# Batches in groups of 2, 4, 4, 4, 2 with a table for each group, in a two-layer graph kernel

## The chip, the core and the metric

The kernel runs on one core of a Trainium2 chip. The time is device microseconds of one execution; the median of three timed runs is given, and lower is better. One more execution was recorded by the hardware profiler, and all views below are of that one. Engines: PE multiplies matrices, DVE is VectorE, ACT is ScalarE, POOL is GpSimd and issues the indirect DMAs (gathers and scatters), SP issues the plain DMAs.

## What is computed

There are 16 graphs ("batches") of 1024 nodes with 64 channels, `x` (16, 1024, 64), and a sparse weighted adjacency `adj` (16, 1024, 1024), 64 MB in float32. Most nodes have few neighbours; nodes with a low number have many, up to some 88. Two layers:

```python
h = relu(layernorm(x));  x = x + (adj / max(rowsum(adj), 1)) @ h              # layer 0
h = relu(layernorm(x))                                                       # layer 1
adj_d = dilate(adj)     # in rows with over 10 neighbours, every skip-th one is removed, on both sides
agg   = 0.25*q25 + 0.5*q50 + 0.25*q75 of h over the neighbours in adj_d      # per node and channel
x = x + (relu((h + agg) @ W1 + b1) @ W2 + b2) * mask
```

Layer 1 needs, per node and channel, a sort of a list whose length differs from node to node.

## The kernel before

**Layer 0** streams the adjacency once, batch by batch, in 8 row tiles of 128 x 1024. For each tile PE transposes it (`transposes`), ACT copies the transposed blocks out (`turned`) and takes the sign of every entry (`signs`), DVE multiplies the signs by column keys and takes the eight largest of each of four interleaved segments (`listing`, MAX8), which gives the list of neighbours. PE then multiplies (`products`), DVE adds the residual, and `channels` makes the normed rows of layer 1, which SP writes to a table in DRAM: one table `tab` for all 16 batches, 1025 rows each, with one row of huge values for empty places.

`endings` gives every node of a batch a place in the order of list lengths (`to`, DVE) and scatters its record (normed row, residual, list) to that place of the group's DRAM tensor `srt[g]`: 8 indirect DMAs of POOL for a batch.

**A group** is four batches (`GB`). When all four are scattered, `group(g)` loads the records sorted by length as 32 tiles of 128 nodes. Tile 0 holds the longest lists of every batch, and is left to `long_lists`. For the other 31, `CAPS` says how many neighbours each holds: 15, 10, 8, 7, 7, 6, and so on down to 1. The group also fetches 128 adjacency rows (`gat_rows`), scans them, and writes with two small scatters ("drops") into the table what each of the longest nodes removes; the gathers of layer 1 must see that.

**A job** (`Job`) takes the tiles of one cap, T of them, with n - 1 neighbours: POOL gathers one neighbour for 128 nodes with each indirect DMA (`places`), DVE works out which are removed (`rem`, `gone`, `ok`, `valid`) and the weights (`q`, `wu`, `w`), adds a huge value to removed ones, and runs a sorting network of `tensor_tensor` min and max between `places` and `other`; the result is weighted (`prod`), summed by PE, run through the two small matrices (`layers`) and scattered to the output by POOL (`out_dram`). Four `places` buffers exist. With `helped`, ACT adds the huge value and does part of the weighting, in pieces of 64 elements; before, that is so once all 16 batches are done.

**Long lists** (`long_lists`) are four jobs with 88, 31, 24 and 20 neighbours for 8 nodes of each batch, after layer 0. They gather from `tab` too (`lplaces`).

**The order.** All this is written as generators ("streams"). A planner (`Plan`) keeps a clock for every engine and for DMA, estimates when each tile is ready (`note`, `ready`, `used`), and always emits the stream that can begin earliest, with ranks to break ties. On DVE and POOL the instructions run in exactly the order in which the planner emits them; a wait at the head of POOL's queue holds everything behind it. `SLACK`, `LOOSE` and `LATE` are what it adds to be safe. An indirect DMA is reckoned with 1.27 us on POOL and 2.2 us to landing. The helper through which the planner records instructions is line 226, so most lines of the profile have that line, and tiles tell them apart.

Since the planner reckons `ready` and `used` for the table as a whole, a gather seems to it to wait for the latest row written by layer 0, and the next write of layer 0 for the latest gather.

Of the kernel before, what the change touches and what calls it, by code (L numbers as in the profile page):

```python
# [18 lines left out]
P = 128  # L19
# [8 lines left out]
GB = 4  # L28
SUB = 32
# [4 lines left out]

CAPS = (
    [0, 15, 10, 8, 7, 7, 6] + [5] * 4 + [4] * 4 + [3] * 6 + [2] * 6 + [1] * 5
)
LONG = (88, 31, 24, 20)
# [193 lines left out]
class Plan:  # L232
# [4 lines left out]
    def __init__(self, nc):  # L237
        names = {"vector": "DVE", "scalar": "ACT", "tensor": "PE", "gpsimd": "POOL", "sync": "SP"}
        self.nc = SimpleNamespace(
            **{attr: Timed(self, name, getattr(nc, attr)) for attr, name in names.items()}  # L240
        )
        self.clock = dict.fromkeys([*names.values(), "DMA"], 0.0)
        self.ready, self.used, self.users = {}, {}, {}
        self.slots, self.streams = {}, []
        self.last = self.own = None

# [21 lines left out]
    def note(self, engine, op, args, kwargs):  # L268
        if self.own is not None:
            self.clock[engine] = max(self.clock[engine], self.own)  # L270
        out = kwargs["out"] if "out" in kwargs else args[0]
        rest = [*args[0 if "out" in kwargs else 1:], *(v for k, v in kwargs.items() if k != "out")]
        rest = [getattr(v, "ap", v) if type(v).__name__.startswith("Indirect") else v for v in rest]
        rest = [v for v in rest if isinstance(v, bass.AP)]
        size = max(math.prod(v.shape[1:]) for v in (out, *rest[:2]))
        start = max(
            self.clock[engine],
            *(self.ready.get(v.tensor.name, 0.0) for v in rest if self.own is None),
            self.used.get(out.tensor.name, 0.0) if self.own is None else 0.0,
        )  # L280
        after = 0.15
        if engine == "DVE":
            half = op == "tensor_tensor" and all(v.dtype == HF for v in (out, *rest))
            time = 0.04 if op == "memset" else 0.07 + size * (0.57e-3 if half else 1.04e-3)
        elif engine == "ACT":
            pointers = sum(isinstance(kwargs.get(k), bass.AP) for k in ("bias", "scale"))
            time = 0.06 + size * 0.86e-3 + 0.11 * pointers + 0.09 * ("accum_out" in kwargs)
        elif engine == "PE":
            time = 0.1 + math.prod(out.shape[1:]) * 0.88e-3
            if op == "matmul" and rest[0].dtype == F32:  # L290
                time *= 2
        elif engine == "POOL":
            time, after = (1.27, 2.2) if op == "indirect_dma_start" else (0.15, 0.1)
            self.last = None
        else:
            start = max(start, self.clock["DMA"])
            rate = 165e3 if 4 * out.shape[-1] >= 512 else 85e3
            time, after = 0.05, 2.2 + math.prod(out.shape) * 4 / rate
            self.clock["DMA"] = start + after - 2.2
        self.clock[engine] = end = start + time  # L300
        self.ready[out.tensor.name] = end + after
        for v in rest:
            self.used[v.tensor.name] = max(self.used.get(v.tensor.name, 0.0), end + after)
        if "accum_out" in kwargs:
            self.ready[kwargs["accum_out"].tensor.name] = end + after
        return start
# [59 lines left out]
def list_path(ctx, tc, x, adj, nodemask, w1, b1, w2, b2, out, go):  # L366
# [7 lines left out]
    NG = B // GB  # L374
# [7 lines left out]
    NTAU = N // SUB  # L382
# [45 lines left out]
    which = consts.tile([P, 2], I32, name="which")  # L428
    nc.vector.tensor_scalar(which[:, 1:2], part, 3, None, op0=OP.logical_shift_right)
    nc.vector.tensor_scalar(which[:, 0:1], which[:, 1:2], GB - 1, None, op0=OP.bitwise_and)  # L430
    toff = consts.tile([P, 2], F32, name="toff")
    nc.vector.tensor_scalar(toff, which, float(TS), None, op0=OP.mult)
    noff = consts.tile([P, 2], F32, name="noff")
    nc.vector.tensor_scalar(noff, which, float(N), None, op0=OP.mult)
    caps = consts.tile([P, NTAU], F32, name="caps")
    for t, cap in enumerate(CAPS):
        nc.vector.memset(caps[:, t:t + 1], float(cap if t else N))
# [28 lines left out]
    tab = dram.tile([B * TS, W], F32, name="tab")  # L466
    srt = [dram.tile([GB * N, RW], F32, name=f"srt{g}") for g in range(NG)]
# [3 lines left out]
    nc.sync.dma_start(tab.rearrange("(b t) w -> b t w", t=TS)[:, N, :], none)  # L471
    pairs = tab.rearrange("r (a two) -> (r a) two", two=2)
# [5 lines left out]
    plan = Plan(nc)  # L478
    nc = plan.nc
# [224 lines left out]
    def channels(pool, now):  # L704

        for b, st in enumerate(batch):
            now[0] = b
            row = lambda: st["row"]
            yield "DVE", lambda: known(st, "row") if st["residual"] == 2 else INF
            yield from normed(row()[:, :, :C], row()[:, :, X1:R0])  # L710
            nc.sync.dma_start(
                tab[b * TS:b * TS + N, :].rearrange("(t p) w -> p t w", p=P), row()[:, :, :W]
            )
            st["normed"] = True

    def endings(pool, now):

        first = lambda rank: rank - 3000
        for b, st in enumerate(batch):
            now[0] = b  # L720
            g, gb = divmod(b, GB)
# [20 lines left out]
            for s in STEPS[1:]:  # L742
# [26 lines left out]
            nc.vector.tensor_scalar(low, low, LSUB - 1, None, op0=OP.bitwise_and)  # L769
            nc.vector.tensor_scalar(  # L770
                pos, pos, float(GB), float(LSUB * gb), op0=OP.mult, op1=OP.add
            )
            to = new(pool, [P, NT], I32, "to", 2)
            nc.vector.scalar_tensor_tensor(to, low, float(1 - GB), pos, op0=OP.mult, op1=OP.add)
# [26 lines left out]
    class Job:  # L801
# [3 lines left out]
        def __init__(self, pool, n, T, keys, idx, node, mask, nodes_i, table, S, g, name="places",  # L805
                     bufs=4, rank=0):
# [3 lines left out]
        def run(self):  # L810
# [6 lines left out]
                at(self.idx), room(self.name, self.bufs), room("S", 4) if short else 0.0  # L817
# [8 lines left out]
            for t in range(T):  # L826
                for k in range(n - 1):
                    if t or k:
                        yield "POOL", pace, *own
                    since.append(since[0] if since else plan.clock["POOL"])  # L830
                    gather(A[:, k + 1, t, :], self.table, self.idx[:, t, k:k + 1])
                    progress["ahead"] -= 1
# [17 lines left out]
        def sort(self):  # L850
# [31 lines left out]
            helped = progress["batches"] == B  # L882
# [82 lines left out]
            helped = progress["batches"] == B  # L965
# [41 lines left out]
        def layers(self, terms, sources):  # L1007
# [55 lines left out]
            for t in range(T):  # L1063
                yield "POOL", lambda: at(y) + LATE
                scatter(out_rows, y[:, t, :], self.nodes_i[:, t:t + 1], scatters)
# [3 lines left out]
    def group(g):  # L1069


        yield "SP", lambda: 0.0 if progress["batches"] >= (g + 1) * GB and (
            g < 2 or progress["jobs"][g - 2] == len(set(CAPS[1:]))
        ) else INF
        R = (g + 1) * GB
        table = tab[:R * TS, :]
        recs = new(grp, [P, NTAU, REC], F32, "recs", 2)
# [8 lines left out]
            nodes, node, noff[:, 0:1], float(g * GB * N), op0=OP.add, op1=OP.add  # L1086
        )
        nodes_i = new(grp, [P, NTAU], I32, "nodes_i", 2)
# [7 lines left out]
        found = new(grp, [P, N], BF, "gfound", 1).rearrange("p (t e) -> p t e", t=NTAU)  # L1096
# [7 lines left out]
        nc.vector.memset(over[:, 0:1], 0.0)  # L1104
        big = tiny.tile([P, NTAU], F32, name="big")
        nc.vector.tensor_tensor(big, m, caps, OP.is_gt)
# [3 lines left out]
        base = tiny.tile([P, 1], F32, name="gbase")  # L1110
        nc.vector.tensor_scalar(base, toff[:, 0:1], float(g * GB * TS), None, op0=OP.add)
# [6 lines left out]
        keys = new(grp, [P, NTAU, 16], F32, "keys", 2)  # L1118
        nc.vector.memset(keys, 0.0)
        left = tiny.tile([P, 8 * NSEG], F32, name="left")  # L1120
        for t in range(1, NTAU):
            nc.vector.max(out=keys[:, t, :8], in_=lists[:, t, :])
            if CAPS[t] > 8:
# [7 lines left out]

        assert all(cap <= T_THRESH for cap in CAPS[2:])
        skip = dilation(m[:, 1:2], mask[:, 1:2], 1)
        hit = tiny.tile([P, 2, 16], F32, name="hit")
        for e in range(2):
# [3 lines left out]
            nc.vector.tensor_tensor(hit[:, e, :], hit[:, e, :], keys[:, 1, :], OP.mult)  # L1139
        nc.vector.tensor_reduce(drop[:, 1, :], hit, AX.X, OP.add)  # L1140
        nc.vector.tensor_scalar(
            drop[:, 1, :], drop[:, 1, :], -1.0, float(N), op0=OP.mult, op1=OP.add
        )
        for e in range(2):
            nc.vector.tensor_tensor(keys[:, 1, :], keys[:, 1, :], hit[:, e, :], OP.subtract)
        didx = new(tiny, [P, 2], I32, "didx", 2)
        index_of(didx, node[:, 0:2], float(PW), basep)
        idx = new(grp, [P, NTAU, 16], I32, "idx", 2)
# [17 lines left out]
        for e in range(2):  # L1166
            nc.gpsimd.indirect_dma_start(
                out=pairs[:R * TS * PW, :],
                out_offset=bass.IndirectOffsetOnAxis(ap=didx[:, e:e + 1], axis=0),
                in_=drop[:, e, :], in_offset=None,  # L1170
            )
        classes = []
        for t in range(1, NTAU):
            if classes and CAPS[t] == CAPS[classes[-1][0]]:
# [3 lines left out]
        for i, ts in enumerate(classes):  # L1178
            n, T = CAPS[ts[0]] + 1, len(ts)
# [3 lines left out]
                nodes_i[:, sl], table, tiles[:, sl, :R0], g,  # L1183
            )
# [3 lines left out]
    def long_lists(pool):  # L1188
# [4 lines left out]
        for l, K in enumerate(LONG):  # L1193
# [3 lines left out]
            n32 = GB * LSUB  # L1197
            for g in range(NG):
                nc.sync.dma_start(
                    S[g * n32:(g + 1) * n32, 0, :], srt[g][l * n32:(l + 1) * n32, :]  # L1200
# [57 lines left out]
            for e in range(2):  # L1258
# [9 lines left out]
                pool, n, 1, keys, idx.unsqueeze(1), node, mask, nodes_i, tab, S, NG,  # L1268
                *(("lplaces", 2) if l else ("lplaces0", 1)), -600 + l,
# [4 lines left out]
    for g in range(NG):  # L1274
# [10 lines left out]
    with tc.tile_pool(name="long", bufs=1) as pool:  # L1285
        plan.add(long_lists(pool), -1500)
# [293 lines left out]
```

## Time and profile before

| | |
|---|---|
| median of 3 runs | 1524.7 us (1523.92 to 1529.08) |
| profiled execution | 1525.97 us, span 1523.8 us |
| DVE busy | 1211.9 us (80%), 4119 instructions |
| POOL busy | 960.8 us (63%), 931 indirect DMAs among 1156 instructions |
| ACT busy | 752.9 us (49%) |
| PE busy | 751.5 us (49%) |
| DMA | 129.01 MB, mean 85 GB/s |
| last scatter of rows (end of layer 0) | issued at 790.9 us |

Issue time on POOL isn't counted as busy, so a POOL that never stops shows some 75 to 80%. The slices of the page are 38.1 us each.

### The profile page before, as it was taken

The page shows a single profiled execution, that of the slowest core. Times are in us where ns is not written, and L with a number is a line of the kernel's source. Part 1 is how long each engine was busy: PE and PEld are TensorE (multiplying, and loading weights), DVE is VectorE, ACT ScalarE, POOL GpSimd, SP SyncE. Part 2 cuts the span into 40 slices and gives each one's busy share as a digit, 9 for nine tenths or more (in the row PEclk, how much of TensorE's full clock was granted, in tenths as well). Part 3 has the DMA queues.
Part 4 walks back from the last instruction along what each step waited for, and adds up shares of the span by engine and source line. Part 5 has one row for each costly group of instructions (what it writes and reads, how often), then busy time and mean ns, then how long its engine had stood idle before and what let it go on. Part 6 is the DMA issues. An engine that isn't in the chain of part 4 may idle for free. (4 is left out here: it accounts for less than half of the span.)

```text
span 1523.8 us, 15747 instructions
## 1 busy us (share of the span) xinstructions
PE 751.5 (49%) x3192; PEld 469.3 (31%) x3192; DVE 1211.9 (80%) x4119; ACT 752.9 (49%) x2503; POOL 960.8 (63%) x1156
## 2 busy tenths in 40 slices
PE   4887776576348777655825420013000056706454
PEld 2443342344214453432413320012000034605343
DVE  6878798999997699999734779995189999998852
ACT  7989878476436665675515320011410147516442
POOL 0122237745567766556677776567777777777774
PEclk8889987787568778767865655555555556857666
DMA  4555764455514354643322131221111111112110
GB/s 153 172 163 156 185 187 116 131 134 172 113 40 104 114 144 129 161 131 83 87 52 37 29 78 34 50 41 31 33 23 24 26 27 30 37 30 45 36 27 17
DMA packets 135536, 129.01 MB, mean 85 GB/s; under 512 B 100696, under 2 KB 103384, under 8 KB 135432
## 3 DMA queue, kind: packets, MB, share of 16 engines
q1 hardware_dynamic: 102696, 86.46, 20.6%
q0 software_dynamic: 32736, 41.47, 12.6%
q14 instruction: 76, 0.62, 0.1%
q8 instruction: 28, 0.46, 0.1%
HBM read 108.57 MB, written 19.28 MB: 84 GB/s over the span
## 5 line engine op out<-in xcount | busy, mean ns | idle before, releaser
L226 POOL DMA_INDIRECT places<-tab,idx x496 | 495.0, 998 | 161.2 <-issue 142.3
L226 PE MATMUL pt<-ident,prod 128*128 128x128 f32 (+1 forms) x736 | 159.1, 376 | 454.0 <-DVE prod L226 369.6
L226 PEld LDWEIGHTS pt<-ident,prod 128*128 128x128 f32 (+1 forms) x736 | 129.4, 257 | 486.1 <-ACT prod L226 287.8
L226 PE MATMUL ps_small<-att,h 128*65 128x512 f32 x512 | 255.4, 649 | 26.9 <-ACT h L226 22.4
L226 POOL DMA_INDIRECT srt<-row,to x128 | 129.6, 1013 | 208.8 <-ACT row L226 186.7
L226 PE MATMUL pt<-ident,at 128*128 128x128 f32 x1024 | 181.0, 324 | 106.7 <-ACT att L226 79.2
L226 POOL DMA_INDIRECT lplaces<-tab,lidx x163 | 166.9, 1024 | 53.7 <-issue 49.1
L226 PEld LDWEIGHTS pt<-ident,at 128*128 128x128 f32 x1024 | 138.5, 166 | 154.2 <-ACT att L226 104.8
L226 DVE MAX8 rec<-sg 128x8 f16<-128x256 f16 x512 | 180.1, 414 | 4.4
L226 ACT ACTIVATE sg<-at 128x1024 f16<-128x1024 f32 x128 | 135.1, 1056 | 69.4 <-DMA at<-in_adj_dram 48.8
L226 ACT COPY att<-pt 128x512 f32<-128x512 f32 x256 | 141.4, 583 | 28.4 <-PE pt L226 27.3
L226 POOL DMA_INDIRECT out_dram<-y,nodes_i x124 | 121.8, 983 | 37.9 <-issue 20.0
L226 PEld LDWEIGHTS ps_small<-att,h 128*65 128x65 f32 x512 | 75.7, 153 | 166.8 <-issue 127.6
L226 ACT ACTIVATE gone<-gone 128x18 f32<-128x18 f32 (+9 forms) x23 | 4.8, 208 | 234.1 <-DVE ok L226 234.1
L226 DVE TENSOR_TENSOR sg<-sg,keyed 128x1024 f16<-128x1024 f16 x128 | 87.4, 683 | 30.4 <-ACT sg L226 30.4
L226 DVE TENSOR_TENSOR long_other<-lplaces 128x512 f32<-128x512 f32 (+5 forms) x124 | 63.8, 557 | 21.8 <-ACT lplaces L226 21.6
L226 PE MATMUL ps_small<-ot,w_sb 128*128 128x128 f32 (+3 forms) x112 | 53.1, 564 | 53.3 <-ACT ot L226 22.5
L226 ACT COPY ot<-pt 128x128 f32<-128x128 f32 (+3 forms) x56 | 22.2, 396 | 109.6 <-PE pt L226 109.3
L226 DVE TENSOR_TENSOR other<-places,other 128x64 f32<-128x64 f32 (+6 forms) x204 | 69.6, 341 | 5.9
L226 ACT ACTIVATE places<-places,gone 128x64 f32<-128x64 f32 x283 | 70.7, 335 | 0.4
L226 ACT ACTIVATE prod<-places,w 128x64 f32<-128x64 f32 x157 | 39.5, 335 | 63.1 <-DVE w L226 63.1
L226 DVE TENSOR_TENSOR places<-places,other 128x64 f32<-128x64 f32 (+2 forms) x208 | 62.4, 310 | 4.9
(210 smaller groups left out, 1643.3 us busy)
## 6 DMA issues: line engine op xcount, KB each, us to landing
at<-in_adj_dram SPq DMA_DIRECT2D x128, 512.0 KB
places<-tab,idx POOLq DMA_INDIRECT x496, 2.5
tab<-row SPq DMA_DIRECT2D x16, 264.0 KB
xt<-in_x_dram SPq DMA_DIRECT2D x16, 256.0 KB
lplaces<-tab,lidx POOLq DMA_INDIRECT x163, 2.5
recs<-srt SPq DMA_DIRECT2D x4, 544.0 KB
srt<-row,to POOLq DMA_INDIRECT x128, 2.7
out_dram<-y,nodes_i POOLq DMA_INDIRECT x124, 2.2
```

The source lines that it names most:

```text
L226: ins = getattr(self._engine, op)(*args, **kwargs)
```

## The change

1. **Groups.** Five groups of 2, 4, 4, 4 and 2 batches. A group of two has 16 tiles; its first tile is shared, half for long lists and half for short ones of cap 15 (`HP`, `half`, `aside`), and its caps are `CAPS2`. There are 48 jobs of short lists instead of 40. The preparation of the last group is added with the long lists, after layer 0.
2. **A table for each group** instead of one `tab`, and `whole`, a copy of all of them that only the long lists gather from. SP copies each group's table there after the group's drops have landed (DRAM to DRAM). In a group of two one drop is enough.
3. **The plan.** A gather is put down at POOL's clock, without waiting for its table; writes of a table's parts neither wait for one another nor move its `ready`; DMA with small pieces keeps the DMA clock busy for half as long.
4. **`helped`** now holds for any job for which ACT's clock is less than 2 us ahead of DVE's, during layer 0 too.

```diff
-GB = 4
-SUB = 32
+GROUPS = (2, 4, 4, 4, 2)
...
+CAPS2 = [CAPS[1]] + CAPS[2::2]
...
         after = 0.15
+        apart = engine == "SP" and out.tensor.name in self.parts
+        if apart:
+            start = max(self.clock[engine], *(self.ready[v.tensor.name] for v in rest))
...
-            rate = 165e3 if 4 * out.shape[-1] >= 512 else 85e3
-            time, after = 0.05, 2.2 + math.prod(out.shape) * 4 / rate
-            self.clock["DMA"] = start + after - 2.2
+            busy = math.prod(out.shape) * 4 / 165e3
+
+            time, after = 0.05, 2.2 + busy * (1 if 4 * out.shape[-1] >= 512 else 2)
+            self.clock["DMA"] = start + busy
         self.clock[engine] = end = start + time
-        self.ready[out.tensor.name] = end + after
+        if not apart:
+            self.ready[out.tensor.name] = end + after
...
-    tab = dram.tile([B * TS, W], F32, name="tab")
-    srt = [dram.tile([GB * N, RW], F32, name=f"srt{g}") for g in range(NG)]
+    tabs = [dram.tile([n * TS, W], F32, name=f"tab{g}") for g, n in enumerate(GROUPS)]
+    whole = dram.tile([B * TS, W], F32, name="whole")
+    srt = [dram.tile([GROUPS[g] * N, RW], F32, name=f"srt{g}") for g in range(NG)]
...
+            if size == 2:
+                aside = new(tiny, [P, 2, NT], F32, "aside", 2)
+                for e, by in enumerate((-32.0, 64.0)):
+                    nc.vector.tensor_scalar(
+                        aside[:, e, :], pos, 64.0 / (e + 1), by, op0=OP.is_lt, op1=OP.mult
+                    )
+                for e in range(2):
+                    nc.vector.tensor_tensor(pos, pos, aside[:, e, :], OP.add)
...
+                    plan.own = plan.clock["POOL"]
                     gather(A[:, k + 1, t, :], self.table, self.idx[:, t, k:k + 1])
+                    plan.own = None
...
-            helped = progress["batches"] == B
+            helped = plan.clock["ACT"] < plan.clock["DVE"] + 2.0
...
-        for e in range(2):
-            nc.gpsimd.indirect_dma_start(
-                out=pairs[:R * TS * PW, :],
+        for e in range(2 if four else 1):
+            if e:
+                nc.gpsimd.memset(turn, 0.0)
+            ins = nc.gpsimd.indirect_dma_start(
+                out=table.rearrange("r (a two) -> (r a) two", two=2),
                 out_offset=bass.IndirectOffsetOnAxis(ap=didx[:, e:e + 1], axis=0),
                 in_=drop[:, e, :], in_offset=None,
             )
+            if e:
+                tc.declare_no_dep(ins.ins, other, reason="rows of their own")
+            other = ins.ins
+        dropped = at(table)
+        yield "SP", lambda: dropped
+        nc.sync.dma_start(whole[FIRST[g] * TS:R * TS, :], table)
...
-    for g in range(NG):
+    for g in range(NG - 1):
         plan.add(group(g), -2000)
...
     with tc.tile_pool(name="long", bufs=1) as pool:
+
+        plan.add(group(NG - 1, pool, "last_"), -2000)
         plan.add(long_lists(pool), -1500)
```

## The prediction

> **What bounds the kernel now.** I read the page's busy shares and slices first, then the waits of POOL and of VectorE, then POOL's timeline, whose rows I counted. The slices:
>
> ```profile
> DVE  6878798999997699999734779995189999998852
> ACT  7989878476436665675515320011410147516442
> POOL 0122237745567766556677776567777777777774
> ```
>
> POOL is empty in the first 65 us, and from slice 20 on it stands at 7 of 10 without a gap. Seven tenths is its full pace, as the timeline shows (start, duration, idle time before):
>
> ```profile
> 1082.49 0.94 POOL L226 DMA_INDIRECT lplaces<-tab,lidx  x1 [0.30 <-issue]
> 1083.73 0.95 POOL L226 DMA_INDIRECT lplaces<-tab,lidx  x1 [0.30 <-issue]
> 1084.99 0.94 POOL L226 DMA_INDIRECT lplaces<-tab,lidx  x1 [0.30 <-issue]
> ```
>
> One indirect DMA costs a slot of 1.25 us, 0.94 busy and 0.30 of issue. Summed over all 931, with the small memsets between scatters, slots take 1,222 us, 1.307 each; real waits take the other 302 us: 162 us before time 200, 97 from 200 to 800, 43 after. So after layer 0 the queue of POOL sets the end, and before it whatever makes gathers available.
>
> ```profile
> POOL srt L226 <- ACT row L226: 186.7, 24, 64.7
> POOL tab L226 <- DVE deg L226: 17.5, 1, 17.5
> POOL gat_rows L226 <- DVE nodes_i L226: 14.6, 1, 14.6
> ```
>
> These are POOL's longest waits: scatters that wait for a batch's rows (132 of the 186.7 us before time 200), then the preparation of the first group. The first group's gathers start at 214.7, because four batches must be sorted first (last scatter at 174.1):
>
> ```profile
> 174.14 0.96 POOL L226 DMA_INDIRECT srt<-row,to  x1 [0.19 <-issue]
> 189.71 1.17 POOL L226 DMA_INDIRECT gat_rows<-in_adj_dram,nodes_i  x1 [14.61 <-DVE nodes_i L226]
> 208.41 0.98 POOL L226 DMA_INDIRECT tab<-drop,didx  x1 [17.54 <-DVE deg L226]
> 212.35 0.96 POOL L226 DMA_INDIRECT tab<-drop,didx  x1 [2.96 <-DMA tab<-drop,didx]
> 214.71 0.97 POOL L226 DMA_INDIRECT places<-tab,idx  x1 [1.40 <-DMA tab<-drop,didx]
> ```
>
> VectorE is the second bound: its instructions, each to the start of the next where that follows at once, add up to 1,211 us (layer 0 425, jobs of short lists 415, long lists 290, preparation of groups 81), and 296 us of waits.
>
> **What the Trainium skill says.** "DMA: Bandwidth & Descriptors", section on the anatomy of a DMA on the gpsimd path, puts most of about 2 us of fixed cost into the receipt at the end, which the issuing queue sees only when something waits for it. The trace agrees: the second drop above starts 3.9 us after the first, a gather behind a gather 1.25 us. "SBUF — State Buffer", section "Who interferes with whom", says that VectorE instructions with two SBUF inputs contend with GpSimd reads. Here POOL's slot is 1.25 us from 850 to 900 and 1.45 from 1100 to 1150, where VectorE sorts the 88-long lists without a pause; I keep the measured slots by stage. "ScalarE: Activation LUTs", rules for kernel authors, prices an ACTIVATE at some 0.3 us plus 0.83 ns per element, 0.35 us for 64; measured 0.333.
>
> **The change part by part.** The order of the changed program, each form at its mean duration in the trace of before, gives:
> - POOL: 955 indirect DMAs for 931: gathers 518 for 496 (three groups of 124, two of 73), one more adjacency gather, one more output scatter. 24 x 1.307 = +31 us.
> - VectorE: 48 jobs of short lists for 40, so smaller tiles with the same fixed part: jobs 415 to 443 us, preparation 81 to 91, the rest +5: 1,255 us, +43. The multiplication taken over by ScalarE in 23 more jobs is in it (-15 us, 17 to 2 instructions).
> - ScalarE: 217 more value and 76 more product ACTIVATEs. Back to back they take 0.25 us each (283 of them 70.7 us), +73 us; with the small pieces of eight more jobs 763 to 852. It has over 740 us of waits, but it is 86% busy before time 200.
> - SP: five copies of a table into the common one, 0.54 or 1.08 MB. Nothing in the trace copies DRAM to DRAM; the nearest, 512 KB of adjacency, streams at 150 to 185 GB/s, so 6 to 14 us each in the background. Each waits for the drops of its group, and adjacency loads stand behind it in SP's queue. For groups 0 and 1 eight rows or more are issued ahead of what VectorE has reached; for group 2 one row (94 issued, 93 listed). That hold costs nothing at the low end (VectorE has sorts to do), some 20 us of layer 0 at the high end; I take 0, the long one is in the range.
> - A drop no longer waits for all gathers issued before it (the one table made it wait on all eight DMA semaphores of POOL's queue). In the trace only the second drops show it: 3.0 + 1.9 + 1.4 + 1.4 us. Worth 5 us at most.
>
> Now POOL's queue by stages of the new order. First gather: it needs two batches; the second one's last scatter ends at 109 in the trace of before. Preparation takes 36 us (214.7 - 174.1, less one drop): 145.
> Second group: batches 2 to 5. VectorE's work up to the sixth batch's positions is 255 us, its waits by then were 42: 297; ScalarE reaches its rows at 264 + 37 = 301. Fifteen output scatters stand before its eight scatters on POOL and need the last job of group 0 (VectorE 247 + 42, then PE and ScalarE): about 305 + 23 x 1.3 = 335. Records, positions, scan: 25 us: 360. POOL has 132 DMAs between 145 and there, 173 us, so 42 us idle.
> From there to the end of layer 0 (issue 150 to 544): 394 x 1.307 = 515, plus waits. VectorE has 459 us of work in that stretch, and sets when groups 2 and 3 are ready within 10 to 15 us of when POOL gets to them: 25 us of waits. 900. (Layer 0 ended at 792 before, with 120 gathers fewer done.)
> To the last of the 88 long gathers (544 to 691): 147 x 1.28 (that stage's slot) = 188, waits 29, as much as before had from 900 to 1100 beyond what the early stage explains (22) and one more group's chain: 1117.
> Then 249 DMAs to the last gather of the last long list. The trace has 248 between the same two points (1085.0 to 1422.7), 338 us, 1.36 each: 339. 1456.
> The last job is now a 20-long list: landing 3 us, sort 27 (1430.8 to 1457.6 in the trace), ScalarE and PE 10, scatter 1.5, and 8.6 from the last issue to the end: 50. Before, the last gather was 40 us from the end.
> Sum 1,506 us of span. The profiled execution took 1525.97 with a span of 1523.8 (+2.2), and is 1.3 above the median of 1524.7: 1,507 in a timed run.
>
> Where the stall goes: the second group starts 72 us earlier (360, for 432 before), but 43 more DMAs stand behind that point (805 for 762, 56 us), and the tail is 13 us longer for what it holds. What is left of the gain comes from the waits between that point and the tail, 54 us for 70: -72 + 56 + 13 - 16 = -19.
>
> **The rivals.** *POOL never dry*: the gathers of groups 2 and 3 are always ready, waits 0 and 10 us instead of 25 and 29, the second group starts at 345. 145 + ... = 345 + 515 + 198 + 339 + 50 = 1,447; with half of it 1,475, which I take as its value. For it: between 450 and 600 before, POOL waited under 9 us. Against: VectorE's load grows too.
> *Nothing measurable*: the second group starts at 375 because ScalarE, with 30 us of help in the stretch 150 to 300 where it was 57 to 84% busy, makes rows later: 1,522 to 1,528. It includes the case that the changed order does not remove the waits.
> *Slower, by ScalarE's help*: a helped job sends VectorE's values to ScalarE and back. Before, only the 23 jobs behind layer 0 did, with ScalarE a third busy, and VectorE waited 27 us for it, 1.2 us a job:
>
> ```profile
> DVE other L226 <- ACT places L226: 23.6, 6, 6.5
> DVE places L226 <- ACT places L226: 3.1, 2, 2.0
> ```
>
> In layer 0 ScalarE has signs of 1.06 us and copies of 0.58 us in its queue. VectorE has 540 - 459 = 81 us of slack there, over some 25 helped jobs: from 3.2 us a job on it is the bound. At 5 us: 125 - 81 = +44: 1,550. At the longest single wait, 6.5: 1,588. For it: the order lets other work of VectorE stand between, which hid it before.
>
> **How the numbers follow.** Forecast (1,490 to 1,520): 0.47. POOL never dry: 0.15. Nothing measurable: 0.14. Slower: 0.24. No change can be told from within 0.3%, 1,520 to 1,529. Faster 0.62, same 0.14, slower 0.24. The range, 1,455 to 1,555, leaves out the upper half of the slow case and the extreme of the good one.
>
> **What would show it.** In the changed kernel's timeline: first gather near 145, second group's near 360, last scatter of rows near 900, last long gather near 1117, last gather near 1456. POOL's slots 1,250 us, waits about 260. VectorE 1,250 us of busy time. A wait of VectorE for `places` from ScalarE over 80 us, or for adjacency rows behind a table copy, would make it wrong on the slow side; a last row scatter before 870 on the fast side.

## The result, and the profile after

The changed kernel takes 1581.04 us (median of four runs, 1580.33 to 1582.06), the kernel before 1524.97 beside it: a ratio of 1.0363, 95% interval 1.0343 to 1.0383. It is 56 us slower; the forecast was 1,507. The profiled execution has a span of 1580.3 us, 56.5 more than before. The last ten experiments below fell on chips on which every kernel, the one before too, took about 1.3 times as long; they are read only by their ratio to the kernel before on the same chip, or against a neighbour there.

The slices of the changed kernel's page, 39.5 us each:

```profile
DVE  6869899578899986599857928969706999989975
ACT  7977857587767638557775640001104012591731
POOL 0222776333767777775675774476777777777562
```

POOL is at its pace from slice 4 on (158 us), and then falls back to 3 of 10 for three slices, 276 to 395 us. It falls again in slices 24 and 25, from 948 us on, and at the end. Before, it rose more slowly, and from slice 6 on it stood at 4 to 7.

A gather still costs the slot it cost before, as POOL's timeline shows:

```profile
1129.51 0.94 POOL L228 DMA_INDIRECT lplaces<-whole,lidx  x1 [0.30 <-issue]
1130.76 0.95 POOL L228 DMA_INDIRECT lplaces<-whole,lidx  x1 [0.30 <-issue]
```

The first group is ready where the prediction put it (145 us): its last row scatter, the adjacency rows, the one drop and the first gather.

```profile
110.27 0.96 POOL L228 DMA_INDIRECT srt<-row,to  x1 [0.19 <-issue]
128.59 0.97 POOL L228 DMA_INDIRECT gat_rows<-in_adj_dram,nodes_i  x1 [17.36 <-DVE nodes_i L228]
144.15 1.26 POOL L228 DMA_INDIRECT tab<-drop,didx  x1 [14.58 <-DVE ln_v L228]
146.84 0.97 POOL L228 DMA_INDIRECT places<-tab,idx  x1 [1.44 <-DMA tab<-drop,didx]
```

POOL's waits, summed by what ended them (total us, times, longest):

```profile
POOL srt L228 <- ACT row L228: 120.0, 13, 62.7
POOL out_dram L228 <- DVE y L228: 57.8, 9, 21.5
POOL gat_rows L228 <- DVE nodes_i L228: 42.6, 3, 17.4
...
POOL lplaces L228 <- DVE lnodes L228: 16.2, 1, 16.2
```

The waits for rows fell from 186.7 to 120.0 us, as meant. In their place stand waits for outputs of jobs (57.8, of which 31.5 at the first group's last jobs; 10.8 before) and for the start of a group (42.6; 14.6 before). POOL's timeline shows where the large ones before time 400 lie:

```profile
326.17 0.96 POOL L228 DMA_INDIRECT out_dram<-y,nodes_i  x1 [15.39 <-DVE y L228]
...
345.80 1.00 POOL L228 DMA_INDIRECT srt<-row,to  x1 [13.34 <-ACT row L228]
...
369.72 1.18 POOL L228 DMA_INDIRECT gat_rows<-in_adj_dram,nodes_i  x1 [14.04 <-DVE nodes_i L228]
...
388.27 0.96 POOL L228 DMA_INDIRECT tab<-drop,didx  x1 [6.21 <-DVE found L228]
389.53 0.96 POOL L228 DMA_INDIRECT tab<-drop,didx  x1 [0.19 <-issue]
```

The second group's second drop is at 389, forecast for 360; a group's drop below means this second one. Counting all of POOL's instructions as the prediction did, with each wait put down to the time at which it begins, beside the run with four groups of four that follows (e2):

| POOL | before | after | groups of 4, 4, 4, 4 |
|---|---|---|---|
| indirect DMAs issued by 200 us | 33 | 60 | 33 |
| by 400 us | 151 | 156 | 173 |
| left to issue at 800 us | 519 | 516 | 473 |
| waits up to 200 us | 162 | 120 | 169 |
| waits from 200 to 400 | 40 | 75 | 8 |
| waits from 400 to 800 | 57 | 33 | 28 |
| waits after 800 | 43 | 100 | 91 |
| slots, all | 1,222 | 1,253 | 1,217 |

27 DMAs' worth of early start has shrunk to 5 by 400 us. At 800 us both kernels have about as much left; the changed one then loses 57 us in waits, since three batches of layer 0 are still to come (its last row scatter is at 949 us, before at 791) and the last group and the long lists are prepared behind them.

### The profile page after: what moved, and what is told of

The parts are those of the page before. It is cut to its first block, busy times and chain, and to the rows that moved or that the text cites. A ratio compares the mean times of both kernels' runs of the same rounds, so it can differ in the third digit from the quotient of the medians.

```text
span 1580.3 us, 16506 instructions
## 1 busy us (share of the span) xinstructions
PE 786.0 (50%) x3234; PEld 499.9 (32%) x3234; DVE 1247.2 (79%) x4402; ACT 832.0 (53%) x2853; POOL 984.9 (62%) x1181
## 5 line engine op out<-in xcount | busy, mean ns | idle before, releaser
L228 POOL DMA_INDIRECT places<-tab,idx x445 | 444.6, 999 | 155.4 <-issue 122.9
L228 PE MATMUL pt<-ident,prod 128*128 128x128 f32 (+1 forms) x756 | 172.6, 388 | 457.5 <-DVE rem L228 205.1
L228 PEld LDWEIGHTS pt<-ident,prod 128*128 128x128 f32 (+1 forms) x756 | 139.3, 267 | 492.5 <-ACT prod L228 240.3
L228 PE MATMUL ps_small<-att,h 128*65 128x512 f32 x512 | 252.0, 640 | 37.1 <-ACT h L228 23.6
L228 POOL DMA_INDIRECT lplaces<-whole,lidx x163 | 167.3, 1026 | 65.6 <-issue 47.3
L228 POOL DMA_INDIRECT out_dram<-y,nodes_i x109 | 108.4, 995 | 58.2 <-DVE y L228 35.8
L228 ACT ACTIVATE prod<-places,w 128x64 f32<-128x64 f32 x233 | 59.1, 335 | 157.6 <-DVE w L228 157.6
L228 DVE TENSOR_TENSOR sg<-sg,keyed 128x1024 f16<-128x1024 f16 x128 | 87.4, 683 | 68.4 <-ACT sg L228 68.4
L228 ACT ACTIVATE places<-places,gone 128x64 f32<-128x64 f32 x500 | 126.8, 335 | 0.6
L228 PE MATMUL ps_small<-ot,w_sb 128*128 128x128 f32 (+4 forms) x122 | 57.5, 569 | 113.9 <-ACT places L228 50.1
L228 POOL DMA_INDIRECT places<-tab,last_idx x73 | 73.2, 1003 | 36.8 <-issue 19.2
L228 DVE TENSOR_TENSOR places<-places,other 128x64 f32<-128x64 f32 (+5 forms) x242 | 69.8, 298 | 5.6
```

Of the source, the lines that this page charges most:

```text
L228: ins = getattr(self._engine, op)(*args, **kwargs)
```

## The experiments

The theories: **W**, the groups of two cost the work that they add, wherever they stand; **S**, it is their early start; **H**, ScalarE's help; **C**, the copies in SP's queue; **P**, the plan; **Y**, the residual loads in SP's queue. Ratios are to the kernel before on the same chip, with 95% intervals.

### One part undone: e1 to e4

Help only behind layer 0, at both places:

```diff
-            helped = plan.clock["ACT"] < plan.clock["DVE"] + 2.0
+            helped = progress["batches"] == B
```

> The changed kernel with ScalarE's help again only behind layer 0, all else as changed. Theory H (the help makes ScalarE's and TensorE's queues wait for VectorE in layer 0, so that tiles of adjacency come free late): most of the 74 us by which the forecast was missed come back, the second group's drop at 365 or earlier (389 in the changed kernel), layer 0 done by 910 (949), 1,505 to 1,530 us. Theory G (groups of two), theory C (copies of tables in SP's queue) or theory P (the plan): VectorE gets some 15 us more of work and nothing else moves, second drop at 380 to 400, 1,575 to 1,600 us.

1600.5 us, 1.0505 (1.0486 to 1.0524): 20 us slower than with the help. H falls. The second group's drop stays at 392, and VectorE has 37 us more to do; the busy lines of this run and of the changed kernel:

```profile
PE 764.5 (48%) x3234; PEld 484.1 (30%) x3234; DVE 1283.9 (80%) x4460; ACT 709.3 (44%) x2313; POOL 989.8 (62%) x1177
```

```profile
PE 786.0 (50%) x3234; PEld 499.9 (32%) x3234; DVE 1247.2 (79%) x4402; ACT 832.0 (53%) x2853; POOL 984.9 (62%) x1181
```

```diff
-GROUPS = (2, 4, 4, 4, 2)
+GROUPS = (4, 4, 4, 4)
```

> The changed kernel with groups of 4, 4, 4, 4, all else as changed: tables, copy, plan and help stay. Theory G (48 jobs for 40, small tiles, 24 more indirect DMAs, a second preparation in the busiest stretch): 1,515 to 1,535 us, with 931 indirect DMAs. Theories H, C and P: the first gather comes some 65 us later again (near 212), and the cause of the loss stays, so 1,590 to 1,630 us.

1514.8 us, 0.9939 (0.9920 to 0.9958): 0.6% faster than the kernel before, and 66 us faster than the changed one. The spans of the two profiles are 67.7 apart, of which POOL's slots are 37 (24 fewer DMAs) and its waits 31. The loss of the change lies in its groups of two; in this order its other parts together gain 10 us. Its slices show that POOL holds its pace from slice 6 on, and where it loses again, at the end:

```profile
POOL 0122227777677767757777787667777777765073
```

The one long wait there is the output of a long list, which VectorE has not finished; the last long list is gathered behind it:

```profile
1392.09 0.11 POOL L228 MEMSET turn<- 128x1 f32 x1
1428.45 0.96 POOL L228 DMA_INDIRECT out_dram<-y,lnodes_i  x1 [36.25 <-DVE y L228]
1435.76 0.97 POOL L228 DMA_INDIRECT lplaces<-whole,lidx  x1 [6.35 <-PE pt L228]
```

At 800 us this run is 46 DMAs ahead of the kernel before; 48 us of that go into waits after 800.

```diff
+        def copied():
-        yield "SP", lambda: dropped
-        nc.sync.dma_start(whole[FIRST[g] * TS:R * TS, :], table)
+            yield "SP", lambda: dropped if progress["batches"] == B else INF
+            nc.sync.dma_start(whole[FIRST[g] * TS:R * TS, :], table)
+            progress["whole"] += 1
+        plan.add(copied(), -1800)
...
```

> The changed kernel with the five copies of tables into the common one issued only when layer 0 is over, each as a stream of its own. Theory C (a copy that waits for its drops at the head of SP's queue holds loads of adjacency; SP waited 80 us so in the changed kernel): 1,525 to 1,550 us, no wait of SP for drops before the end of layer 0. Theories H, G and P: the hold is only where loads run ahead of what is needed, 1,570 to 1,583 us.

1562.4 us, 1.0252 (1.0233 to 1.0271): 19 us less than the changed kernel, between the two theories. The second group's drop is at 374. But here VectorE and POOL got another order too, which g1 below separates.

The plan as before (no `plan.own` around a gather, `plan.parts` left empty, the old DMA rate):

```diff
-                    plan.own = plan.clock["POOL"]
                     gather(A[:, k + 1, t, :], self.table, self.idx[:, t, k:k + 1])
-                    plan.own = None
...
```

> The changed kernel with the planner's reckoning as before: a gather waits for its table, writes of a table wait for one another, small pieces keep the DMA clock busy twice as long. Theory P (the plan without false waits sends out gathers and jobs earlier than VectorE and ScalarE can take them, to the cost of layer 0): 1,525 to 1,550 us and layer 0 done earlier than 949. Theories H, G and C: the plan gains what it was reckoned to, so 1,585 to 1,620 us.

1580.3 us, 1.0361 (1.0341 to 1.0380): no different from the changed kernel. P falls, and so does the idea that the plan brings a gain of its own in this kernel.

### Single parts, and the place of the small groups: e5 to e9

> The kernel before with one part of the change alone: ScalarE's help for any job for which its clock is less than 2 us ahead of VectorE's, in layer 0 too. The rival of the prediction (the help makes VectorE wait for ScalarE, from 3.2 us a job on a loss): slower than 1,525, up to 1,550. What the run without help in layer 0 says (the changed kernel lost 19 us without it): 1,500 to 1,518 us, VectorE's busy time down by 25 us or more, and its waits for places from ScalarE below 80 us.

The two `helped` lines of the change, put into the kernel before: 1534.4 us, 1.0059 (1.0038 to 1.0081). A loss of 0.6%, 7 to 9 us, though VectorE's busy time falls by 17 (1211.9 to 1194.6). Here VectorE does wait for ScalarE's values, 64.1 us for 23.6:

```profile
DVE other L226 <- ACT places L226: 64.1, 14, 10.9
```

In the changed kernel the same wait is 7.2 us in all:

```profile
DVE other L228 <- ACT places L228: 7.2, 3, 3.2
```

> The changed kernel with groups of 4, 4, 4, 2, 2 batches: still two groups of two, so 48 jobs and 955 indirect DMAs, but none of them early; first gather near 215 (147 in the changed kernel). Theory W (the groups of two cost the work of 8 more jobs and 24 more indirect DMAs, wherever they stand): 1,570 to 1,590 us. Theory S (it is the early start: jobs of the first group in the stretch where layer 0 is the bound, whose order then holds adjacency back): 1,530 to 1,550 us, sixth batch scattered near 270 (355), end of layer 0 before 920 (949).

`GROUPS = (4, 4, 4, 2, 2)`: 1585.8 us, 1.0402 (1.0370 to 1.0435). W, not S. The first gather is at 217, layer 0 goes as in e2 (sixth batch scattered at 269, e2 270), by 400 us 173 DMAs are issued, and yet the time is that of the changed kernel: an early start is worth nothing in the end. POOL's slots are 42 us above e2's, its waits 28, all of these after 800 us; what causes these waits is open.

> The changed kernel, with the residual of a job loaded into its y buffer only when TensorE has the job's product, not when the job's turn on TensorE begins; so these loads stand in SP's queue later. Theory Y (loads into y that wait for the landing of older output scatters hold the adjacency loads behind them: 16.5 us of SP's queue in the stretch 180 to 320, 272 us in all): 1,550 to 1,570 us, and the seventh batch's last tile loaded before 300 (315). Theories W and S: 1,575 to 1,590 us.

```diff
-            yield "PE", lambda: max(at(*sources) + LOOSE, room("y", 6), room("pt", 2))
+            yield "PE", lambda: max(at(*sources) + LOOSE, room("pt", 2))
-            y = new(mlp, [P, T, CO], F32, "y", 6, users=1)
-            x1 = y
-            if self.short:
-                nc.sync.dma_start(x1, self.residual)
...
+                if not t0:
+                    yield "SP", lambda: max(at(py), room("y", 6))
+                    y = new(mlp, [P, T, CO], F32, "y", 6, users=1)
+                    x1 = y
+                    if self.short:
+                        nc.sync.dma_start(x1, self.residual)
...
```

1569.8 us, 1.0282 (1.0260 to 1.0303), 11 us below the changed kernel. But the second group's drop stays at 394 and the seventh batch's last tile at 316: the gain isn't where Y puts it, so Y isn't what delays the second group.

> The changed kernel with two parts altered: groups of 4, 4, 4, 4, and the copies of tables issued behind layer 0. If the two gains seen alone (66 and 19 us) are separate: 1,490 to 1,502 us. If the copy costs only where the small groups have made layer 0 short of adjacency: 1,510 to 1,518 us.

1547.0 us, 1.0132 (1.0090 to 1.0175): 32 us *worse* than e2. The copies that gained 19 us late in one kernel lose 32 in another. Neither expectation holds: the parts don't add up. It also bears on the size of W: with late copies the groups of two cost only 15 us (e3 against e9), with early ones 66. That they cost time shows in both orders, how much does not. Each edit also makes the planner set the streams in another order; the next runs keep it.

### Orders kept, or nothing but the order changed

Here the planner notes what it noted before, so that VectorE and POOL keep the changed kernel's order, while the instruction itself is moved or left out.

> The changed kernel with its order on VectorE and GpSimd kept: the planner notes each copy of a table where it did, but SP issues the copies of the first groups only behind layer 0. If the 19 us that the late copies gained came from SP's queue (adjacency no longer stands behind a copy that waits for its drops): 1,558 to 1,568 us. If they came from another order of the streams: 1,575 to 1,584 us.

```diff
...
+        if progress["batches"] < B:
+            plan.note("SP", "dma_start", (part, table), {})
+            held.append((part, table))
+        else:
-        nc.sync.dma_start(part, table)
+            nc.sync.dma_start(part, table)
...
         plan.run(lambda: progress["batches"] == B)
+        for part, table in held:
+            tc.nc.sync.dma_start(part, table)
```

> The changed kernel in its own order, with the sorting networks of the first group's jobs left out (two memsets a job in their place, so the values of that group are not sorted): some 50 us less work of VectorE between 185 and 290. If VectorE sets when the second group is ready: its drop at 350 or earlier (389), 1,535 to 1,555 us. If it is the chain of adjacency loads, TensorE and ScalarE: drop at 375 to 390, 1,565 to 1,581 us.

```diff
...
+                if short and self.g == 0:
+                    plan.note("DVE", "tensor_tensor", (dst, a, c, op), {})
+                else:
-                nc.vector.tensor_tensor(dst, a, c, op)
+                    nc.vector.tensor_tensor(dst, a, c, op)
```

> The changed kernel in its own order, with 24 gathers of the second group's first two jobs (between 390 and 450) left out, a memset of GpSimd for each job in their place: 29 us less of POOL's queue in layer 0. If POOL's queue sets the pace there, as the prediction's sum had it: 1,549 to 1,558 us, end of layer 0 at 920 to 925 (949). If layer 0's own engines do and POOL's waits only grow: 1,572 to 1,582 us, layer 0 done at 940 to 950.

```diff
...
+                    if self.g == 1 and (n == 16 and k or n == 11):
+                        plan.note("POOL", "indirect_dma_start", (), dict(
+                            out=A[:, k + 1, t, :], in_=self.table, at=self.idx[:, t, k:k + 1],
+                        ))
+                    else:
-                    gather(A[:, k + 1, t, :], self.table, self.idx[:, t, k:k + 1])
+                        gather(A[:, k + 1, t, :], self.table, self.idx[:, t, k:k + 1])
```

> The changed kernel with one constant of the planner altered, the allowance LATE 15 for 14, no work added or removed: how much the order by itself is worth. If differences between runs are those of their parts: 1,577 to 1,585 us. If a nearly equal order can be worth as much as the help or the copy: 10 us or more away from 1,581, on either side.

`LATE = 15.0` in the changed kernel.

These four took 2,021 to 2,050 us where the kernel before took 1,963, so their expected times, which reckon with 1,525, say nothing here. The first three follow again, with a fourth, on another chip, where the kernel before took 1,966:

> The changed kernel in its own order on VectorE and GpSimd, with SP issuing the copies of the first groups' tables only behind layer 0; the same kernel as f1_copy_fixed, for a chip on which the kernel before takes some 1,525 us. If the copies' hold on adjacency costs: 1,558 to 1,568 us. If the 19 us of the late copies came from another order: 1,575 to 1,584 us.

> The changed kernel in its own order with the sorting networks of the first group's jobs left out, the same kernel as f2_no_net0. If VectorE sets when the second group is ready: its drop at 350 or earlier (389) and 1,535 to 1,555 us. If it is adjacency, TensorE and ScalarE, whose order was planned for VectorE's work: drop at 375 to 390, 1,565 to 1,581 us. Of the disturbed chip, where the drop moved by 6 us: the second.

> The changed kernel in its own order with 24 gathers of the second group left out, the same kernel as f3_no_24: what 24 indirect DMAs are worth when they stand in layer 0. If POOL's queue sets the pace there: 1,549 to 1,558 us. If layer 0's own engines do and POOL's waits grow by as much: 1,572 to 1,582 us.

> The changed kernel with groups of 4, 4, 4, 4 and one constant of the planner altered, LATE 15 for 14: no work added or removed against the run e2_groups4 (1,515 us). If an order by itself is worth little: 1,511 to 1,519 us. If nearly equal orders differ as much as the late copies made this kernel differ (32 us): anywhere from 1,500 to 1,550 us, and 10 us or more from 1,515.

`LATE = 15.0` with groups of four. The last two runs put the changed kernel itself beside one of them (1,999 us before):

> The changed kernel itself, for the runs that kept its order. On a chip like the first: 1,578 to 1,584 us. On a chip like that of the last eight runs: 2,030 to 2,055 us; then the runs with its order stand beside it: if the copies' hold cost, it is 15 us or more above g1_copy_fixed (2,052 us), and if 24 gathers cost what they take on POOL, some 29 us or more above g3_no_24 (2,016 us).

> The changed kernel in its own order with 24 gathers of the second group left out, on the same chip as the changed kernel beside it. If POOL's queue sets the pace of layer 0, as the prediction's sum had it: 24 to 33 us less than the changed kernel. If layer 0's own engines do and POOL's waits grow by as much: within 9 us of it.

| | ratio to before | 95% |
|---|---|---|
| changed kernel (a1) | 1.0380 | 1.0341 to 1.0420 |
| copies late, order kept (f1, g1) | 1.0423, 1.0463 | 1.0342 to 1.0503, 1.0433 to 1.0493 |
| first group's networks out (f2, g2) | 1.0379, 1.0379 | 1.0296 to 1.0462, 1.0330 to 1.0428 |
| 24 gathers out (f3, g3, h3) | 1.0305, 1.0279, 1.0190 | 1.0232 to 1.0378, 1.0252 to 1.0306, 1.0152 to 1.0228 |
| LATE 15, changed kernel (n1) | 1.0316 | 1.0245 to 1.0388 |
| LATE 15, groups of four (n2) | 1.0033 | 1.0002 to 1.0064 |

- **24 gathers**: a1 and h3 ran on one chip, 2076.0 and 2038.5 us, 37.5 apart; POOL's slots fall by 32 us (1,240 to 1,208). In the two profiles the third group's drop comes 25 us earlier (736 to 711) and layer 0 ends 25 us earlier (1231 to 1206). The profiled executions are 22 us apart, since POOL's waits are 10 us longer in h3's: most of what is taken out of POOL's queue in layer 0 is not swallowed by its waits. This is one part of W, its DMAs, seen singly.
- **Networks of the first group**: VectorE does 43 us less (1,251 in a1, 1,208 in g2), and the ratio is that of a1. The second group's drop moves from 449 to 435 us (g2, on another chip), 14 of the 29 us by which it missed the forecast on the first chip. VectorE's load is at most a part of what delays the second group, and less of it makes the whole no faster.
- **Copies**: with the order kept, moving them out of SP's way gains nothing. C falls on these chips, which leaves the order of the streams for e3's 19 us; that is argued from the first chip's run and these, not shown on one chip.
- **Order alone**: n1's ratio is 0.6% below that of a1, and their intervals overlap: by these intervals one draw is worth no more than some 1.5%. n2 stands at 1.0033 where e2 stood at 0.9939; across kinds of chips that difference can't be given to the order. How much an order alone is worth was not measured on a chip like the first.

## Why the prediction was wrong

**What held.** The first gather (145; measured 146.8), POOL's slots (1,250; 1,253), VectorE's busy time (about 1,250; 1,247), its time for the sixth batch's positions (297; 295), the price of 24 more DMAs (+31; slots rose by 32). The two drops of a group of four now follow each other after 1.26 us, 3.9 before: the receipt, into which the Trainium skill ("DMA: Bandwidth & Descriptors", section "Anatomy of one DMA — SWDGE (gpsimd) path") puts most of a DMA's fixed cost, does not show in POOL's queue once nothing waits for it. The copies of tables cost nothing that the runs with the order kept show (taken at 0).

**The step that failed** is "Second group", and in it one clause: "ScalarE reaches its rows at 264 + 37 = 301". The clause before it held: VectorE has the sixth batch's positions (`to`) at 295, forecast for 297. But ScalarE makes that batch's normed rows at 345: its work by then is 265 us, as put down, and its waits 80 instead of 37. So the last of its scatters starts at 355 (254 before) where the sum was done with them at 335, the preparation behind them takes 34 us for 25, and the drop is at 389 for 360; POOL waits 75 us on the way for 42. The sum adds up each engine's own work and the waits that it had before (42 us for VectorE, 37 for ScalarE); it has no term for a longer wait of the rows on the other engines. A row needs TensorE's products of adjacency and normed `x` (`h`), and `h` came late:

```profile
295.22 0.17 DVE L228 SCALAR_TENSOR_TENSOR to<-low,pos 128x8 int32<-128x8 int32 x1
296.52 0.17 DVE L228 TENSOR_TENSOR ln_s<-ln_s,ln_v 128x8 f32<-128x8 f32 x1
297.50 2.74 ACT L228 ACTIVATE h<-xt,ln_s,ln_v 128x64 f32<-128x64 f32 x8
303.69 7.08 PE L228 MATMUL ps_small<-att,h 128*65 128x512 f32 x16
311.29 1.07 ACT L228 COPY att<-pt 128x512 f32<-128x512 f32 x2
345.09 2.75 ACT L228 ACTIVATE row<-row,ln_s,ln_v 128x64 f32<-128x64 f32 x8
```

In the kernel before, the same batch's `h` begins at 164 (in e2 at 160), and its products at 192:

```profile
163.81 0.76 ACT L226 ACTIVATE h<-xt,ln_s,ln_v 128x64 f32<-128x64 f32 x2
```

The sixth batch's `x` was loaded at 128, and its adjacency transposed by 263; VectorE's order has the last step of the statistics of `x` (`ln_s`) at 296.5, with the first group's preparation and jobs set before it. The products then last until 328, the residual and the rows' own statistics until 345.

Layer 0's stream of adjacency stops at the same link. The transposed blocks (`att`, two buffers) are held until the products have read them, so ScalarE copies none for the seventh batch between 263 and 311, its row tiles stay in their five buffers, and SP can load no more. The seventh batch's last tile is issued at 315, in e2 and e7, where no small group comes first, at 228 and 227. The seventh batch belongs to the third group: the stop is not what delays the second group's drop, but it holds back the batches behind. SP's timeline of the changed kernel shows it:

```profile
213.31 2.99 SPq L228 DMA_DIRECT2D at<-in_adj_dram  x3
...
261.87 1.20 SPq L228 DMA_DIRECT2D at<-in_adj_dram  x2
...
285.18 1.20 SPq L228 DMA_DIRECT2D y<-srt  x2
297.23 0.30 SPq L228 DMA_DIRECT2D mrow<-in_nodemask_dram  x1
311.02 8.82 SPq L228 DMA_DIRECT2D at<-in_adj_dram  x5
```

No adjacency is issued between 263 and 311. Two stretches of 50 us, first of the changed kernel, then of e2 (window, its length, then busy us and count of PE, weight loads, DVE, ACT, POOL, granted clock, DMA share, GB/s):

```profile
250.00:300.00 50.00, 34.86 (x122) 24.99 (x123) 42.52 (x168) 32.83 (x123) 28.51 (x40) 0.53 0.24 63
300.00:350.00 50.00, 44.71 (x189) 22.88 (x189) 27.58 (x86) 40.73 (x128) 14.55 (x26) 0.98 0.41 125
```

```profile
250.00:300.00 50.00, 21.02 (x96) 15.42 (x94) 43.69 (x169) 30.53 (x106) 38.86 (x47) 0.67 0.46 128
300.00:350.00 50.00, 20.98 (x71) 12.65 (x72) 47.08 (x168) 29.16 (x108) 39.09 (x47) 0.58 0.27 68
```

From 300 to 350 VectorE is busy for 28 us of 50 in the changed kernel and POOL for 15; in e2 both work on. Over the whole run VectorE waits for ScalarE's signs 68.4 us, 30.4 before:

```profile
DVE sg L228 <- ACT sg L228: 68.4, 23, 11.1
```

Undoing the help, the copies in SP's way, the plan or the early residual loads (e1, e3, e4, e8) leaves the drop at 374 to 394. In each of these kernels `h` of the sixth batch is late too (295, 282, 267, 299), and adjacency is issued again 14 to 19 us after it; in e4 the rows come late a second time, at 341 with the products done at 306. With the order kept and the first group's networks left out (g2 beside a1, on another chip), `h`, the next load of adjacency and the drop all come 13 to 14 us earlier. So the traces name the link, the place of the sixth batch's `x` in VectorE's order; no run moved it alone, so what it costs in the end is not shown, and why the planner put it there is open.

**The steps built on it** failed by less each, and on the same side: to the end of layer 0 POOL waited 45 us where 25 were put down (949 us for 900); to the last of the 88 long gathers 42 for 29 (1,179 for 1,117); the next 249 DMAs took 348 us for 339; the tail 53.3 for 50. 29 + 20 + 13 + 9 + 3 = 74 us, which is the whole error. So in the closing sum, "-72 + 56 + 13 - 16", the first term was -43, and the gain in waits, -16, was a loss of some 25 to 30: POOL's waits are 327 us in all, 302 before, 260 forecast.

**The rivals.** *Slower, by ScalarE's help*: the side was right and the mechanism wrong. Its point of decision (3.2 us a job) was not reached in the changed kernel, 7.2 us in all, and without the help in layer 0 the kernel is 20 us slower. It is seen where the help stands alone: 64.1 us of that wait and a loss of 7 to 9 us in the kernel before. *POOL never dry*: no; POOL is at 3 of 10 from 276 to 395 us. *Nothing measurable*: its second group at 375 was nearer than 360, but it kept the later steps. A rival was missing: that the early jobs delay the next batches by as much, so that 24 DMAs and 8 jobs remain as pure cost. e7 has that cost without the early start, and takes about the same time (1585.8 us).

**The measure of success** was named too weakly: a "last scatter of rows near 900" was already 109 us later than before, for 120 gathers more. The table shows what to ask instead: how many DMAs are left at a given time.

## What to carry to other kernels

When an in-order queue starves early, feeding it sooner helps only if the stage that feeds it has room: follow the producer's last item through every engine with the new work in its way, rather than adding up each engine's work and the waits it had before, and compare work left at a fixed time rather than the time of the first item. Smaller batches bring fixed parts with them (here 24 indirect DMAs of 1.25 us and 8 jobs), and these stay when the head start is gone; here groups of two cost 15 us in one order and 66 in another. Where a planner lays out the program, an edit also brings a new order, and gains of single edits don't add up; keep the order and leave out the part to tell them apart. The best run here has all of the change but the groups of two: 1514.8 us, 0.9939 of the kernel before; after 1350 us it has 72 us of waits (21 in the kernel before), which was not worked on.

## What the runs showed of the hardware

Not expected: one and the same program took some 1,525 us (the kernel before) on the two chips of e1 to e9 and 1,963 to 1,999 on the three others. On the latter VectorE's gaps of over 0.3 us add up to 735 us in the changed kernel (250 on the first). Among them are rows of gaps of 2 to 3 us between instructions of one list, where the profile shows nothing that is waited for:

```profile
1615.23 0.69 DVE L228 TENSOR_TENSOR long_other<-long_other 128x512 f32<-128x512 f32 x1 [3.04 <-issue]
...
1619.43 0.69 DVE L228 TENSOR_TENSOR lplaces<-long_other 128x512 f32<-128x512 f32 x1 [3.00 <-issue]
```

VectorE's busy time is 1,251 us there and 1,247 on the first chip; POOL's slots add up to 1,240 and 1,253. The mean granted TensorE clock was 0.638 there and 0.678 on the first. Why instructions come late on these chips isn't known.
